# A graph network's edge sums: the first five edge tiles of every source tile moved between the scatter blocks

## The chip, the cores and the metric

The kernel runs on one core of a Trainium2 chip. The metric is the device time of one execution in microseconds: the median of three runs of the kernel before is 2264.07 us (2262.4 to 2264.69). One execution was also profiled; every row shown below is from that one. The core's engines are PE (TensorE, matrix products and transposes), DVE (VectorE), ACT (ScalarE), POOL (GpSimd) and SP (SyncE, which issues transfers here). Each engine works through its own instructions in order; a wait at the head of an engine's queue holds all that stands behind it. "PEld" in the profile is the loading of weights into TensorE.

## The reference, cut to what matters

There are N = 3125 nodes of 256 features, E = 50000 edges (src, dst), sorted by dst, and 16 features per edge. The first half is a message network, the second a graph convolution of three layers:

```python
h = relu(layernorm(x))
z = concat([h[src], h[dst], edge_attr])          # per edge
m = relu(z @ mW1 + mb1) @ mW2 + mb2              # hidden width 512
agg = segment_sum(m, src, N)                     # per source node
u = relu(concat([h, agg]) @ uW1 + ub1) @ uW2 + ub2
x = x + h + u
h = relu(layernorm(x))
# three layers: A_norm @ (h @ W_l) + b_l, gelu between them; edges and self loops
x = x + gcn(h)
```

## The kernel before

**Splitting the message.** mW1 is cut into the part for the source, the part for the destination and the part for the edge's features. The kernel makes two tables, tabA = h times the source part and tabB = h times the destination part plus mb1 (each row is kept as a rounded number and its remainder, 2 × 512 wide). A message's hidden row is relu(tabA[src] + tabB[dst] + edge part), and the sum over a source's edges is taken before mW2 is applied. 25 source tiles of 125 nodes each have 17 edge tiles of 128 places (2176 places in rows_d, each a row of 528 numbers = 2112 bytes).

**Stage one, the blocks.** In a start-up the kernel normalizes nodes (`norm`, `turn_nodes`, which also stores h to h_d), and computes for every edge its place in rows_d (lines 319 to 417: one-hots S of the source tile, counts, prefix sums, peers, place, ends). Then come 66 blocks of 768 edges, six columns of 128 edges each, in the order of dst. `window(b)` (line 526) loads 128 rows of tabB for block b, three blocks ahead; SP issues it, or ACT for every fifth block. `prepare(b)` makes the transposed features and the one-hots of the destinations (lines 540 to 555). `block(b)` makes the products p_z on PE (lines 568, 570), copies them two columns at a time into one of four buffers zt (line 573, ACT for four columns and DVE for two) and sends every column to its places with an indirect transfer from POOL (line 576, `rows_d<-zt,place`, 391 in all). These scatters are declared free of dependencies among each other (the group "rows"), since every edge has a place of its own. Between the blocks the kernel makes the remaining tables (`table`, lines 294 to 311, two chunks of 128 nodes per call), tests on the places (lines 468, 470), stores the transposed h (hT_d), and clears places that may stay empty (`fill`, line 237, two source tiles per transfer). Calls are handed out by block number: what tabB needs in blocks 0 to 17, then the tests, the tables of A and hT in blocks 18 to 61.

**Stage two, the sums** (`messages`, lines 714 to 890). For each source tile t: `load_rows` (line 728) loads its rows in five groups of three or four edge tiles, waiting for all scatters; `load_tile` loads 128 rows of tabA (apc). `one_hots` (lines 750 to 760) makes the one-hot of each edge's source (oh), its transpose (ohT) and a half-precision copy (oh_h). `edge_tile` (lines 799 to 810) picks the row of tabA with the transposed one-hot (p_x), adds the edge's row (gb, DVE), takes the relu (ACT) and the remainder (m, DVE); `sums` (line 818) adds the edge tile into p_sum with the one-hot, and at the end ACT copies p_sum to R (line 822). A list `beside` is handed out between the edge tiles: `adjacency(t - 1)`, which makes one-hots of destinations (od, line 769, DVE) and counts edges into the matrix A (p_A, line 776, and a copy to bytes, line 794), and `update(t - 1)`. The update begins with `edges_of_sources`: POOL adds the 17 one-hot tiles together (lines 832, 835, 836), and a product with a column of ones gives the number of edges of each source. `node_steps` then applies mW2, uW1, uW2. `residual` (called by `fetch`) loads x and h and has POOL add them with the bias ub2 (lines 649, 650).

**Stage three** turns the degree counts into scales and runs the three convolution layers with A (products at line 1097).

**What sets the order.** The order of instructions on each engine is the program's order as the tile framework keeps it, with the lists `of_B`, `work` and `beside` placing the side work by hand. The framework also puts in the waits: an instruction that reads what another writes waits for it, for tiles in memory off the core as well, unless the two were declared free of each other. The line that does this for the scatters, and the wait that row loads of stage two are given by hand:

```python
tc.declare_no_dep(s.ins, group="rows", reason="every edge has a place of its own")
tc.add_to_no_dep_group("rows", s.ins)
...
for s in scatters:
    tc.add_manual_dep(o.ins, s.ins.name, SYNC, reason="all rows are in place")
```

Of the kernel before, what the change touches and what calls it, by code (L numbers as in the profile page):

```python
# [54 lines left out]
EARLY, HEAD, TAIL = 24, 5 * P, 3 * P  # L56
MID = 1024
# [30 lines left out]
assert len(begun) == NG  # L88
FIRST = [v[0][1] for v in PIECES]
# [4 lines left out]
def gnn(ctx: ExitStack, tc: tile.TileContext, x, src, dst, ea, mW1, mb1, mW2, mb2, uW1, ub1, uW2,  # L94
# [11 lines left out]
            dram.tile([N - TAIL, 2 * H], F32, name="tabB1")]  # L106
    hT_d = dram.tile([P, 2, N], F32, name="hT_d")
    h_d = dram.tile([N, D], F32, name="h_d")
# [12 lines left out]
    for name, v, none in (("kr_s", src, -8000), ("kr_d", dst, 0)):  # L121
        t = l1.tile([NB, BLK], I32, name=name)
        nc.vector.memset(t[64:NB, :], none)
        nc.scalar.dma_start(t[:NB - 1, :], v[:FULL].rearrange("(b e) -> b e", e=BLK))
        nc.scalar.dma_start(
            t[NB - 1:NB, :].rearrange("b (p j) -> b p j", j=MB)[:, P - LEFT:, MB - 1:MB],
            v[FULL:].rearrange("(b p j) -> b p j", b=1, j=1))
        kr.append(t)
    xt = g1.tile([P, NR, D], F32, name="xt")
    REST = N - (NR - 1) * P  # L130
    groups = [(0, 5), (5, 13), (13, 19), (19, NR)]
    wAB = g1.tile([P, 2, 2, H], F32, name="wAB")

    def load_x(a, e):
        nc.sync.dma_start(xt[:, a:e, :], x[a * P:e * P, :].rearrange("(c p) f -> p c f", p=P))
# [7 lines left out]
    nc.sync.dma_start(bias_f, mb1.rearrange("(o f) -> o f", o=1))  # L143
# [3 lines left out]
    nc.sync.dma_start(xt[:REST, NR - 1, :], x[(NR - 1) * P:, :])  # L147
    load_w(0)
    wE4 = l1.tile([P, H], F32, name="wE4")
    for q in range(0, P, ED):  # L150
        nc.sync.dma_start(wE4[q:q + ED, :], mW1[2 * D:2 * D + ED, :])

# [60 lines left out]


    scatters = []

    with s1:
# [3 lines left out]
        def small(dtype=F32):  # L221

            turn[0] += 1
            return gps.tile([P, H], dtype, name=("tr", "bc", "p_tab")[turn[0] % 3])
# [7 lines left out]
        zero = g1.tile([P, (KT - SURE // P) * ZW], F32, name="zero")  # L232
# [3 lines left out]
        def fill(a, e, after):  # L236
            f = nc.sync.dma_start(
                rows_d[:ROWS, :].rearrange("(t s) w -> t s w", s=CAP)[a:e, SURE:, :]
                .rearrange("t (p i) w -> p t (i w)", p=P),
                zero.unsqueeze(1).to_broadcast([P, e - a, (KT - SURE // P) * ZW]))  # L240
            tc.add_manual_dep(f.ins, after.ins.name, SYNC, reason="others are wanted first")
            tc.declare_no_dep(f.ins, group="rows", reason="before its places have edges")
            tc.add_to_no_dep_group("rows", f.ins)
            fills.append(f)
# [14 lines left out]
        def norm(c0, c1):  # L259
            for c in range(c0, c1):  # L260
                n = parts(c)
                ln_stats(g1, mv[:n, c, :], xt[:n, c, :], n)
            return ln_scale(g1, mv[:, c0:c1, :], P, f"ln{c0}")

        def turn_nodes(c, e, scale, c0):

            rstd, nmr = scale
            h = g1.tile([P, 2, D], F32, name="h", bufs=3)
            p = small().rearrange("p (k a) -> p k a", k=2)
            for i in range(e - c):  # L270
                n = parts(c + i)
                nc.scalar.activation(h[:n, i, :], xt[:n, c + i, :], AF.Relu,
# [5 lines left out]
            for b, f, n in whole(c, e):  # L278
                a = (c + b) * P
                nc.sync.dma_start(  # L280
                    h_d[a:a + (f - b) * n, :].rearrange("(i p) f -> p i f", p=n), h[:n, b:f, :])
            a, b = c * P, min(e * P, N)
            nc.scalar.copy(hT[:, :, a:b], p[:, :, :b - a])


# [8 lines left out]
        def table(pool, name, s, c, e, stores, bufs=2):  # L294

            p = gps.tile([P, 2, H], F32, name="p_z", bufs=2)
            for i in range(e - c):
                n = parts(c + i)
                if s == 1:
                    nc.tensor.matmul(p[:n, i, :], ones_r[:, :n], bias, start=True, stop=False)  # L300
                for k in range(2):
                    nc.tensor.matmul(p[:n, i, :], hT[:, k, (c + i) * P:(c + i) * P + n],
                                     wAB[:, s, k, :], start=s == 0 and k == 0, stop=k == 1)
            o = pool.tile([P, 2, 2, H], F32R, name=name, bufs=bufs)
            for b, f, n in whole(c, e):
                nc.scalar.copy(o[:n, b:f, 0, :], p[:n, b:f, :])
                nc.vector.tensor_sub(o[:n, b:f, 1, :], p[:n, b:f, :], o[:n, b:f, 0, :].bitcast(F32))
                a = (c + b) * P
                for d, at in stores:
                    d = d[a - at:a - at + (f - b) * n, :].rearrange("(i p) f -> p i f", p=n)  # L310
                    nc.sync.dma_start(d, o[:n, b:f].rearrange("p i s f -> p i (s f)").bitcast(F32))
# [21 lines left out]
        nc.scalar.copy(kd, key_p[1][:, :CN])  # L333
        cs_i = l1.tile([P, CN], I32, name="cs_i")
# [5 lines left out]
        nc.vector.tensor_copy(cs, cs_i)  # L340
        S = l1.tile([P, MB, NT, NB], F16, name="S")
        for t in range(NT):
            nc.vector.tensor_scalar(S[:, :, t, :], cs_h.rearrange("p (j b) -> p j b", j=MB), float(t),
                                    None, op0=ALU.is_equal)
        own = l1.tile([P, NT * NB], F16, name="own")
# [18 lines left out]
        for t0 in range(0, NT, 2 * TG):  # L364
            p = gps.tile([P, 2, H], F32, name="p_z", bufs=2)
            for i in range(2):
                a = t0 + i * TG
                v = slice(a * NB, min(a + TG, NT) * NB)
                n = v.stop - v.start
                nc.tensor.matmul(p[:, i, :n], tri, own[:, v], start=True, stop=False)  # L370
                nc.tensor.matmul(p[:, i, :n], ones_h[:NB, :], Xv[:, v], start=False, stop=True)
                nc.vector.tensor_scalar(base[:, v], p[:, i, :n], float(-MID), None, op0=ALU.add)

        p_pos = gps.tile([P, H], F32, name="p_pos")
# [10 lines left out]
        same = l1.tile([P, CN], F16, name="same")  # L385
        for d in range(1, MB):
            n = (MB - d) * NB
            nc.vector.tensor_tensor(same[:, :n], cs_h[:, d * NB:], cs_h[:, :n], op=ALU.is_equal)
            nc.vector.tensor_add(peers[:, d * NB:], peers[:, d * NB:], same[:, :n])
        real = g1.tile([P, CN], F32, name="real")  # L390
        nc.vector.tensor_scalar(real, cs, -0.5, None, op0=ALU.is_gt)
        pos = g1.tile([P, CN], F32, name="pos")
        nc.vector.scalar_tensor_tensor(pos, real, float(MID), peers, op0=ALU.mult, op1=ALU.add)
        nc.vector.tensor_add(pos, pos, p_pos[:, :CN])

        most = l1.tile([P, MB, NB], F32, name="most")
        nc.gpsimd.memset(most, float(CAP))
        nc.gpsimd.memset(most[:, :, :FROM], float(SURE))
        okay = g1.tile([P, CN], F32, name="okay")
        nc.vector.tensor_tensor(okay, pos, most.rearrange("p j b -> p (j b)"), op=ALU.is_lt)  # L400
        nc.vector.tensor_mul(okay, okay, real)
        at = l1.tile([P, CN], F32, name="at")
        nc.vector.scalar_tensor_tensor(at, cs, float(CAP), pos, op0=ALU.mult, op1=ALU.add)
        nc.vector.tensor_mul(at, at, okay)
# [4 lines left out]
        nc.vector.scalar_tensor_tensor(spare, okay, 0.5, spare, op0=ALU.is_lt, op1=ALU.mult)  # L409
        place = g1.tile([P, MB, NB], I32, name="place")  # L410
        nc.vector.tensor_add(place.rearrange("p j b -> p (j b)"), at, spare)
        ps_f = l1.tile([P, CN], F32, name="ps_f")
        nc.vector.scalar_tensor_tensor(ps_f, cs, -float(NP), ks, op0=ALU.mult, op1=ALU.add)
        ends = g1.tile([P, MB, NB, 2], F32, name="ends")
        for i, v in enumerate((ps_f, kd)):
            nc.vector.tensor_scalar(ends[:, :, :, i], v.rearrange("p (j b) -> p j b", j=MB), 1.0, None,
                                    op0=ALU.add)


        for c, f in pairs(*groups[0]):  # L420
            turn_nodes(c, f, scales[groups[0]], 0)
        for c, f in ((0, 2), (2, 3), (3, 5)):
            table(l1, "b_sb", 1, c, f, [(tabB[0], 0)] + [(tabB[1], TAIL)] * (c >= 3))


        w0 = l1.tile([NB, 1], F32, name="w0")
        at0 = (P - LEFT) * MB + MB - 1
        nc.vector.tensor_scalar(w0, pid[:NB], float(NB - 1), krf[1][:, at0:at0 + 1], op0=ALU.is_equal,
                                op1=ALU.mult)
        nc.vector.tensor_add(w0, w0, krf[1][:, 0:1])  # L430
        w_lo = l1.tile([NB, 1], F32, name="w_lo")
        nc.vector.tensor_scalar(w_lo, pid[:NB], EARLY - 0.5, float(TAIL), op0=ALU.is_gt, op1=ALU.mult)
        w_hi = l1.tile([NB, 1], F32, name="w_hi")
        nc.vector.tensor_scalar(w_hi, w_lo, (N - HEAD) / TAIL, float(HEAD - P), op0=ALU.mult,
                                op1=ALU.add)
        nc.vector.tensor_tensor(w0, w0, w_lo, op=ALU.max)
        nc.vector.tensor_tensor(w0, w0, w_hi, op=ALU.min)
# [766 lines left out]
```

## Time and profile before

| part of the profiled execution | from, us | to, us | length, us |
|---|---|---|---|
| start-up, to the first scatter | 0 | 78.3 | 78.3 |
| blocks 0 to 25 | 79.4 | 353.6 | 274.2 |
| blocks 26 to 65 | 353.6 | 713.7 | 360.1 |
| between the last scatter and the sums | 713.7 | 738.0 | 24.3 |
| sums, 25 source tiles | 738.0 | 1660.0 | 922.0 |
| last update, degrees | 1660.0 | 1687.0 | 27.0 |
| convolution layers | 1687.0 | 2261.0 | 574.0 |
| span | | | 2261.1 |
| this execution's own time | | | 2262.93 |
| median of the runs | | | 2264.07 |

The stages were cut where a line's first or last instruction starts or ends (line 576 for the blocks, lines 750 and 822 for the sums). Over the whole span PE is busy 1910.8 us (85%), DVE 1364.2 (60%), ACT 958.7 (42%) and POOL 566.1 (25%); the shares differ much from stage to stage, so each stage is read for itself. The largest groups of instructions:

| line, engine | what | count | busy, us | mean, ns |
|---|---|---|---|---|
| L576 POOL | scatter of 128 rows | 391 | 378.4 | 968 |
| L1097 PE | convolution products | 2100 | 443.3 | 370 |
| L818 PE | sums, 512 columns | 850 | 355.9 | 458 |
| L803 PE | row of tabA, 512 columns | 850 | 337.0 | 460 |
| L808 DVE | remainder of m | 425 | 313.1 | 745 |
| L805 DVE | gb | 425 | 286.8 | 680 |
| L769 DVE | one-hots of destinations | 425 | 237.0 | 578 |
| L832 POOL | first addition of one-hot tiles | 25 | 56.8 | 2272 |

A matrix product's busy time overlaps its neighbours'; how far two are apart is read from their starts.

### The profile page before, as it was taken

The page shows a single profiled execution, that of the slowest core. Times are in us where ns is not written, and L with a number is a line of the kernel's source. Part 1 is how long each engine was busy: PE and PEld are TensorE (multiplying, and loading weights), DVE is VectorE, ACT ScalarE, POOL GpSimd, SP SyncE. Part 2 cuts the span into 40 slices and gives each one's busy share as a digit, 9 for nine tenths or more (in the row PEclk, how much of TensorE's full clock was granted, in tenths as well). Part 3 has the DMA queues.
Part 4 walks back from the last instruction along what each step waited for, and adds up shares of the span by engine and source line. Part 5 has one row for each costly group of instructions (what it writes and reads, how often), then busy time and mean ns, then how long its engine had stood idle before and what let it go on. Part 6 is the DMA issues. An engine that isn't in the chain of part 4 may idle for free. (4 is left out here: it accounts for less than half of the span.)

```text
span 2261.1 us, 27055 instructions
## 1 busy us (share of the span) xinstructions
PE 1910.8 (85%) x9215; PEld 1489.7 (66%) x9215; DVE 1364.2 (60%) x2863; ACT 958.7 (42%) x1755; POOL 566.1 (25%) x607
## 2 busy tenths in 40 slices
PE   4588767767883889999999999998978999999993
PEld 2455445544552667777777777777756998998991
DVE  8743333333431899999999999999952223223221
ACT  1333222222331555555555555555636444344430
POOL 1355466666563221221212121212100000000000
PEclk9889877789996899999999999999989999999995
DMA  3879898877996454544444444444411000000003
GB/s 127 313 283 344 289 347 305 285 245 255 340 324 221 151 166 138 166 148 153 153 153 148 163 138 165 150 154 153 143 59 50 1 1 1 1 1 1 1 4 112
DMA packets 158307, 358.91 MB, mean 159 GB/s; under 512 B 28643, under 2 KB 55685, under 8 KB 157768
## 3 DMA queue, kind: packets, MB, share of 16 engines
q1 hardware_dynamic: 111066, 235.28, 31.3%
q0 software_dynamic: 31280, 105.73, 12.3%
q10 hardware_dynamic: 15806, 16.01, 2.4%
q8 instruction: 76, 1.25, 0.2%
q14 instruction: 79, 0.65, 0.1%
HBM read 191.45 MB, written 165.44 MB: 158 GB/s over the span
## 5 line engine op out<-in xcount | busy, mean ns | idle before, releaser
L576 POOL DMA_INDIRECT rows_d<-zt,place x391 | 378.4, 968 | 269.1 <-issue 114.7
L1097 PE MATMUL p_o<-a,g 125*128 125x448 f32 x2100 | 443.3, 370 | 0.0
L1097 PEld LDWEIGHTS p_o<-a,g 125*128 125x128 f32 x2100 | 394.8, 188 | 32.5 <-ACT g L1069 0.3
L818 PE MATMUL p_sum<-m,oh 128*125 128x512 f32 x850 | 355.9, 458 | 66.0 <-DVE m L808 46.2
L807 ACT ACTIVATE m<-gb 128x512 fp32r<-128x512 f32 x425 | 265.4, 632 | 233.4 <-DVE gb L805 221.7
L803 PE MATMUL p_x<-apc,ohT 125*128 125x512 f32 x850 | 337.0, 460 | 2.3 <-DVE gb L805 1.1
L808 DVE SCALAR_TENSOR_TENSOR m<-gb,m 128x512 fp32r<-128x512 f32 x425 | 313.1, 745 | 8.2 <-ACT m L807 6.1
L805 DVE TENSOR_TENSOR gb<-z,p_x 128x512 f32<-128x512 f32 x425 | 286.8, 680 | 30.1 <-PE p_x L803 27.1
L570 PE MATMUL p_z<-bw,ohd 128*128 128x512 f32 x782 | 285.5, 449 | 0.0
L1091 DVE CAST a<-A 125x448 fp32r<-125x448 uint8 x262 | 102.9, 393 | 273.6 <-PE p_o L1097 273.5
L568 PE MATMUL p_z<-wE,payT 128*128 128x512 f32 x391 | 186.4, 477 | 76.8 <-issue 27.9
L1093 ACT CAST a<-A 125x448 fp32r<-125x448 uint8 x263 | 148.7, 566 | 240.8 <-PE p_o L1097 240.8
L776 PE MATMUL p_A<-od,oh_h 128*126 128x448 f16 (+2 forms) x1000 | 248.9, 317 | 0.0
L818 PEld LDWEIGHTS p_sum<-m,oh 128*125 128x125 f32 x850 | 154.0, 188 | 142.9 <-DVE m L808 68.3
L573 ACT COPY zt<-p_z 128x1024 f32<-128x1024 f32 x131 | 132.2, 1010 | 256.6 <-PE p_z L570 129.3
L769 DVE TENSOR_SCALAR od<-iota_h,dloc 128x896 f16<-128x896 f16 (+16 forms) x425 | 237.0, 578 | 0.3 <-PE p_A L776 0.3
L570 PEld LDWEIGHTS p_z<-bw,ohd 128*128 128x128 f32 x782 | 169.8, 218 | 76.5 <-issue 45.0
L803 PEld LDWEIGHTS p_x<-apc,ohT 125*128 125x128 f32 x850 | 153.5, 194 | 34.9 <-ACT ohT L759 9.6
L568 PEld LDWEIGHTS p_z<-wE,payT 128*128 128x128 f32 x391 | 84.8, 217 | 131.3 <-issue 56.0
L554 DVE TENSOR_SCALAR ohd<-bc,pid 128x384 fp32r<-128x384 f32 x132 | 81.0, 614 | 131.1 <-PE bc L552 61.7
L776 PEld LDWEIGHTS <-oh_h 128*126 128x126 f16 x1000 | 133.3, 136 | 37.7 <-issue 1.2
L573 DVE COPY zt<-p_z 128x1024 f32<-128x1024 f32 x65 | 79.3, 1221 | 97.3 <-remote 37.6
(225 smaller groups left out, 2263.6 us busy)
## 6 DMA issues: line engine op xcount, KB each, us to landing
z<-rows_d SPq DMA_DIRECT2D x75, 792.0 KB
z<-rows_d SPq DMA_DIRECT2D x50, 1056.0 KB
bw<-tabB SPq DMA_DIRECT2D x53, 512.0 KB
rows_d<-zero SPq DMA_DIRECT2D x12, 1584.0 KB
tabA<-t_sb SPq DMA_DIRECT2D x12, 1024.0 KB
apc<-tabA SPq DMA_DIRECT2D x24, 512.0 KB
tabB<-t_sb SPq DMA_DIRECT2D x9, 1024.0 KB
bw<-tabB ACTq DMA_DIRECT2D x13, 512.0 KB
```

The lines of the kernel that those rows point to most:

```text
L568: nc.tensor.matmul(o, pay[b][:, j // 2, :], wE[j % 2], start=True, stop=False)
L570: nc.tensor.matmul(o, one[b][:, j, :], bw[b][:, s * H:(s + 1) * H], start=False, stop=s == 1)
L573: (nc.vector.tensor_copy if j0 == 2 else nc.scalar.copy)(z[:, a:e, :H], p[:, a - j0:e - j0, :])
L576: s = nc.gpsimd.indirect_dma_start(out=rows_d, in_=z[:, j, :], in_offset=None, out_offset=bass.IndirectOffsetOnAxis(ap=place[:, j, b:b + 1 ...
L769: nc.vector.tensor_scalar(targets[k][:, :WIDTH[k]], iota_h[:, :WIDTH[k]], dloc[t][:, k:k + 1], None, op0=ALU.is_equal)
L776: nc.tensor.matmul(p_A[g][:, l - g * AW:h - g * AW], oh_h[t][:, k, :], targets[k][:, l - FIRST[k]:h - FIRST[k]], start=start, stop=stop)
L803: nc.tensor.matmul(p, ohT, apc[t][:NP, s, :], start=s == 0, stop=s == 1)
L805: nc.vector.tensor_add(gb, zr, p)
L807: nc.scalar.activation(m[:, 0, :], gb, AF.Relu)
L808: nc.vector.scalar_tensor_tensor(m[:, 1, :], gb, 0.0, m[:, 0, :].bitcast(F32), op0=ALU.max, op1=ALU.subtract)
L818: nc.tensor.matmul(p_sum[t], oh, m[:, s, :], start=k == 0 and s == 0, stop=k == KT - 1 and s == 1)
L1097: nc.tensor.matmul(po[:, f, :AW], g[:, s, q, f * P:(f + 1) * P], a, start=s == 0 and q == 0, stop=s == NT - 1 and q == 1)
```

## The change

Stage one also does the first KP = 5 of the 17 edge tiles of every source tile, in blocks FULL_AT = 26 to 65: 125 edge tiles over 40 blocks. By the kernel's own tests these five hold the edges whose destinations are small, so that blocks 0 to 25 fill them. A generator does the work, and is advanced between the blocks:

```diff
+        def rows_of(t):
+            v = g1.tile([P, XZ], F32, name="xz", bufs=2)[:, :KP * ZW]
+            v = v.rearrange("p (k w) -> p k w", w=ZW)
+            o = nc.sync.dma_start(
+                v, rows_d[t * CAP:t * CAP + KP * P, :].rearrange("(k p) w -> p k w", p=P))
+            for c in ready:
+                tc.add_manual_dep(o.ins, c.ins.name, SYNC, reason="all rows are in place")
+            a = p1.tile([P, 2, H], F32R, name="apc", bufs=2)
...
+            nc.sync.dma_start(a.rearrange("p s f -> p (s f)").bitcast(F32)[:n],
+                              tabA[t * NP:t * NP + n, :])
+            return v, a
+
+        def first_sums():
+            loaded = {0: rows_of(0)}
...
+                if k == KP - 1:
+                    r = p1.tile([NP, H], F32, name="R_part")
+                    nc.scalar.copy(r, p_s[t])
+                    nc.sync.dma_start(R_d[t * NP:(t + 1) * NP, :], r)
+            for t in range(NT):
+                if t + 1 < NT:
+                    loaded[t + 1] = rows_of(t + 1)
+                v, a = loaded.pop(t)
...
+                kept = p1.tile([P, KP, NP + 1], F16, name="oh_kept")
+                nc.scalar.copy(kept, oh.bitcast(F32))
+                nc.sync.dma_start(oh_d[t], kept.rearrange("p k n -> p (k n)"))
+                for k in range(KP):
+                    p = gps.tile([P, H], F32, name="p_x", bufs=2)
+                    new = edge_tile(p1, p, ohT[:, k, :], a, v[:, k, :H])
+                    if last is not None:
+                        add(*last)
+                    last = t, k, oh[:, k, :NP], new
+                    yield
...
+            if b == FULL_AT:
+                ready += scatters
+                sums, n_sums = first_sums(), NT * KP
             block(b)
+            for v, n in work:
+                while len(v) > max(0, n - n * (b + 1) // FULL_AT):
+                    v.pop(0)()
+            if b >= FULL_AT:
+                while n_sums > NT * KP - NT * KP * (b + 1 - FULL_AT) // (NB - FULL_AT):
+                    next(sums)
+                    n_sums -= 1
+            if 2 <= b < NT + 2:
+                fill(b - 2, begins[b])
```

So all tables, tests and hT are made by block 25, one chunk of 128 nodes per table call, and the clearing transfers go one source tile per block in blocks 2 to 26. To make room, xt becomes two halves that the rows xz take over later, zt has three buffers in place of four, p_z three single banks in place of two double ones, the features come six blocks at a time. The copies of p_z are made per column, all by ACT from block 26 on (before, DVE makes columns 2 and 3). The one-hots of these five edge tiles (half precision) go to oh_d, the partial sums to R_d, and the destinations' numbers stay on the core (d_of). The manual wait above is for the scatters of blocks before 26.

The residual x + h + ub2 is now made in `turn_nodes` by two DVE additions and stored to xs_d in place of h. In the start-up, several steps move between engines and in order: the peers' sums, `real`, `at` and `ends` go to POOL, `near` to ACT, the first tables and the windows' starts come before the one-hots S, the tests and most `norm` calls come after the first blocks.

Stage two does edge tiles 5 to 16, and has no arithmetic on POOL:

```diff
-        GROUPS = ((0, 4), (4, 8), (8, 11), (11, 14), (14, 17))
+        GROUPS = ((5, 9), (9, 13), (13, 17))
...
+                nc.sync.dma_start(oh_h[t][:, :KP, :].rearrange("p k n -> p (k n)"), oh_d[t])
...
+            def source_counts():
+                nc.tensor.matmul(p_A[g][:, AW:AW + 1], oh_h[t][:, k, :], ones_h[:, 0:1],
+                                 start=False, stop=False)
...
+            if NEW[g]:
+                nc.scalar.copy(of_src[t][:, g:g + 1], p_A[g][:NP, AW:AW + 1])
+            if g == NG - 1:
+                nc.vector.tensor_reduce(n_src[:, t:t + 1], of_src[t], axis=AX.X, op=ALU.add)
...
-                R[t] = mp.tile([NP, H], F32, name="R", bufs=2)
-                nc.scalar.copy(R[t], p_sum[t])
+                nc.vector.tensor_add(R[t], R[t], p_sum[t])
...
-            xs_t[t] = residual(mp, w, t, nc.gpsimd, 3)
+            R[t] = mp.tile([NP, H], F32, name="R", bufs=3)
+            nc.sync.dma_start(R[t], R_d[t * NP:(t + 1) * NP, :])
```

The number of edges of a source is counted on PE, with one product of a single column for each of the 17 edge tiles, into a spare column of p_A; ACT copies seven such columns out and DVE adds them. The partial sums are loaded into R, and DVE adds p_sum to them. The update of a tile comes two tiles later in place of one, and the weights of the update are loaded after the first rows.

## The prediction

> **What bounds the kernel now.** I cut the span by the order of the lines into stages and read each with the windows view (busy time and instructions of each engine, granted clock, DMA share, GB/s): blocks 0 to 25, blocks 26 to 65, the sums stage.
>
> ```profile
> 79.40:353.60 274.20, 208.54 (x739) 136.49 (x738) 108.03 (x247) 83.79 (x110) 151.81 (x157) 0.86 0.85 311
> 353.60:713.70 360.10, 271.34 (x978) 182.84 (x976) 128.75 (x235) 106.66 (x129) 225.44 (x235) 0.88 0.79 283
> 738.00:1660.00 922.00, 848.85 (x4677) 667.56 (x4676) 875.45 (x1727) 514.43 (x1034) 177.07 (x175) 0.98 0.46 149
> ```
>
> The columns are PE, PEld, DVE, ACT, POOL. In the sums stage DVE is busy 875 of 922 us: it is the bound, PE close behind. In the later blocks no engine is full; the timeline shows what paces them:
>
> ```profile
> 374.00 1.01 ACT L573 COPY zt<-p_z 128x1024 f32<-128x1024 f32 x1 [0.32 <-PE p_z L570]
> ...
> 375.21 0.96 POOL L576 DMA_INDIRECT rows_d<-zt,place  x1 [0.30 <-issue]
> ...
> 376.47 0.96 POOL L576 DMA_INDIRECT rows_d<-zt,place  x1 [0.30 <-issue]
> ...
> 377.25 0.39 PE L568 MATMUL p_z<-wE,payT 128*128 128x512 f32 x1
> ...
> 377.49 0.63 PE L570 MATMUL p_z<-bw,ohd 128*128 128x512 f32 x2
> ...
> 377.74 0.96 POOL L576 DMA_INDIRECT rows_d<-zt,place  x1 [0.30 <-issue]
> 377.95 0.40 PE L568 MATMUL p_z<-wE,payT 128*128 128x512 f32 x1
> ```
>
> Scatters start 1.27 us apart (375.21, 376.47, 377.74). 235 of them after block 25 make 298 us of the 360; 62 us are bubbles (waits for the zt copies, mostly). The PE rows give a price used below: three 512-column products from 377.25 to 377.95, 0.23 each. For blocks 0 to 25 the 156 scatters make only 198 of 274 us; with DMA at 0.85 and 311 GB/s I take transfers as their limit.
>
> How DVE loses time in the sums stage:
>
> ```profile
> 1643.17 2.20 POOL L832 TENSOR_TENSOR oh_sum<-oh_h 128x1008 f16<-128x1008 f16 x1 [31.24 <-ACT oh_h L760]
> 1643.32 2.30 DVE L769 TENSOR_SCALAR od<-iota_h,dloc 128x834 f16<-128x834 f16 x1
> ...
> 1645.45 2.65 POOL L835 TENSOR_TENSOR oh_sum<-oh_sum 128x504 f16<-128x504 f16 x3
> 1645.53 1.62 DVE L808 SCALAR_TENSOR_TENSOR m<-gb,m 128x512 fp32r<-128x512 f32 x1
> ```
>
> The 834-wide one-hot takes 2.30 us beside POOL's addition, against about 0.4 by the undisturbed form (1709 columns 0.66 us); L808 takes 1.62 against 0.68. Adding such excesses up gives 4.1 us in each source tile's 36.95 us (24 gaps between the copies of L822, 772.7 to 1659.6).
>
> **The sum, part by part**, against the profiled execution: span 2261.1 us, run 2262.93 (1.8 outside the span); the median of the runs is 2264.07, 0.05% above it.
>
> *Start-up.* The first scatter is at 78.28 now. In the new order 12 of 20 statistics of nodes and the tests stand behind it, the peers' sums go to POOL, the first table comes earlier. 12 × (0.404 + 0.163) = 6.8 us and 7 × 0.555 + 8 × 0.354 = 6.7 us leave DVE; two added additions per pair cost some 1 us back. −12; bounds −18 (more of the chain moved) and −6 (a DMA sets it).
>
> *Blocks 0 to 25.* Now they move 274 × 0.311 = 85 MB. The tables of A (12.8 MB), hT (3.2 MB) and the fills that came later (about 5.7 MB) move in: about 107 to 109 MB. At 335 GB/s (the two fullest slices of the page have 344 and 347) 325 us; at today's 311, 350; at 344, 316. +55, bounds +30 (if part of today's transfers were not the limit) and +80.
>
> *Blocks 26 to 65.* Their engines have room: 125 edge tiles over 40 blocks put PE, ACT and DVE at 7 to 10 us per block, where six scatters take 7.6 and the drains below make it 12. The price is elsewhere. Line 640 of the new kernel loads rows_d while scatters still write it. The scatters are declared free among themselves, the load is not: in the changed kernel's order of instructions each load waits on SP for the last scatter issued before it to land, and the first scatter of the following block waits on POOL for the load. The manual dependency (all scatters of blocks before 26) would ask far less. So the scatter queue is emptied 24 times (tiles 0 and 1 together). Behind the load on SP stand apc, the bw windows (three blocks ahead, so they bear it), R_d and oh_d stores; behind the held scatter stand the rest of POOL's scatters, which set the end. No wait of this kind is in the trace; its parts are. Landing: after the last scatter's issue at 713.74 the next SP transfer starts at 716.14 on its landing, and 1.2 us of this is a recorded wait: 1.4 to 3, taken 2.2. Reading: four edge tiles (512 rows × 2112 B) were issued at 800.57, and the engines worked on them to about 805.4:
>
> ```profile
> 802.00:803.00 1.00, 1.00 (x5) 0.71 (x5) 1.00 (x4) 0.00 (x0) 0.00 (x0) 1.00 0.81 165
> 803.00:804.00 1.00, 1.00 (x7) 0.83 (x7) 0.76 (x4) 0.70 (x2) 0.00 (x0) 1.00 1.04 384
> 804.00:805.00 1.00, 1.00 (x7) 0.77 (x6) 0.98 (x3) 1.00 (x3) 0.00 (x0) 1.00 1.01 367
> 805.00:806.00 1.00, 1.00 (x7) 0.73 (x6) 0.97 (x2) 0.64 (x3) 0.00 (x0) 1.00 0.42 158
> ```
>
> that is 4.8 us, and 128 rows more (0.27 MB at 370 GB/s) make 5.4. With two wakings of 0.1, less the 0.3 between scatters anyway: 7.5 a drain. 24 × 7.5 = 180, and 3.5 for the doubled first load. New: 298 + 180 + 3.5 + 12 (what I leave of the bubbles, since the drains give late copies time to arrive) = 493, so +133. The bytes allow it: 283 GB/s × 360 us = 102 MB, less the A tables, hT and fills, plus rows 33.8, apc 12.8, oh_d 4, R_d 6.4 gives about 144 MB, 430 us at 335 GB/s. Bounds: +110 (the shortest landing, no bubbles) and +170 (today's bubbles in part, landing under load).
>
> [...]
>
> *Gap before the sums* (713.7 to 738.0). The row loads stand ahead of the 2 MB of weights now; the last tile's last sums come in. −7, bounds −12 and 0.
>
> *Sums stage.* Per source tile, now 12 edge tiles. DVE: 12 × (0.60 + 0.60) = 14.4 (clean starts of gb and m), one-hots of targets 6.0, of sources 2.2, the node's 1.0, R's addition 0.6 (as gb's), counts 0.2: 24.4. The 4.1 us beside POOL are gone with POOL's work; if another cause stands behind them they stay, 28.5. PE: 48 products × 0.23 = 11.05, node steps 7.8 and transposes 1.3 (by gaps between starts), counts 6.05, 17 one-column products × 0.064 (line 351 did 25 in 1.6 us) = 1.1: 27.3. ACT about 15: it loses the R copy, gains seven small ones. So PE takes over as the bound. Today's bound, DVE, fills 95% of its stage; with that for PE 27.3 / 0.935 to 27.3 / 0.95, taken 29.2; bounds 27.5 and 31.5 (DVE bound with the stall kept, or coupling of the two). 25 × 29.2 + 32 for the first and last tile's ends = 762, against 949 (738 to 1687): −187, bounds −220 and −130. The gcn stages are untouched.
>
> Sum: −12 + 55 + 133 − 7 − 187 = −18: 2262.9 − 18 = 2245, and 2246 beside the median.
>
> **Rivals.** First, the forecast: the gain of the sums stage slightly exceeds what the blocks give back; its own range, by half the bounds of each term, 2205 to 2259. Second, on the other side: the drain costs more than I priced, at one place, the pair load 640 and the next scatter. The forecast turns at 18 / 24 = 0.75 more, 8.25 us a drain. For it: between loads 9.6 scatters, windows, apc, oh_d and R_d move 4.4 MB in some 12.2 us, 360 GB/s, above anything the page shows, so a backlog would stand before each last scatter and delay its landing; 3.5 us more each (11 us) gives 2246 + 84 = 2330, 1.5 more gives 2282. Against it: apc stands behind the row load on SP and runs while scatters have begun again. Third: PE packs better and DVE's 24.4 + 5% = 25.7 sets the tile: 25 × 3.5 = 88 less, about 2160; against it, PE's 27.3 is already made from back-to-back products. Fourth: the drains fall where the 62 us of bubbles are anyway (both come at ends of blocks), none is left and half of a drain's landing is hidden: 493 − 12 − 24 × 1.1 = 455, 2208; I count it to the forecast's sign. That one-column counts cost more than 0.064 is the small case: at 0.19 each, 2.1 us a tile, +54, on the second's side.
>
> **How the numbers follow.** Forecast 0.42, the second rival (with the last) 0.42, third and fourth together 0.16. About 0.2% (4.5 us) is what a measurement here can tell from no change; 0.06 of the forecast's share falls there. Faster 0.52, within 0.06, slower 0.42. The range leaves out the third's far end and drains above 10.5 us: 2180 to 2320.
>
> **What would show it.** In the changed profile: 24 gaps of about 7.5 us between scatters, each ended by rows loaded; scatters of the later blocks ending about 160 to 175 us later than now; no POOL arithmetic after the blocks and the 834-wide one-hot at 0.4 us; R's addition every 29 us with PE near 94%. I would be wrong on the blocks if scatters ran on through the row loads (then −180), on the sums stage if PE showed idle time behind DVE at a period above 31.5.

## The result, and the profile after

The changed kernel takes 2288.19 us (median of 5 runs, 2278.76 to 2297.84), the kernel before 2264.07 (5 runs, 2258.19 to 2266.63): 1.0105 times the time, with a 95% interval of 1.0066 to 1.0145. The change made the kernel slower by about 1% there; on another chip (e13_after below) the same two kernels are 2.9% apart. The forecast was 2246, a small gain. Of the run e7_poolcounts below, one of the four executions took 4600.51 us, about twice the other three, and is left out of its time.

The profiled execution has a span of 2296.0 us, 34.9 above the span before. The windows view, cut where stages begin and end (first scatter, first scatter of block 26, last scatter's end, first and last addition into R), tells where they come from; the columns are those of the prediction's first view:

```profile
72.07:409.36 337.29, 261.04 (x839) 155.96 (x838) 150.95 (x376) 109.66 (x203) 155.24 (x156) 0.87 0.86 317
409.36:971.80 562.44, 400.75 (x1513) 285.56 (x1512) 249.56 (x513) 267.49 (x495) 237.26 (x235) 0.82 0.71 250
971.80:1016.90 45.10, 29.65 (x145) 21.22 (x145) 29.55 (x69) 18.43 (x39) 0.02 (x1) 0.81 0.77 256
1016.90:1685.80 668.90, 663.97 (x4247) 560.79 (x4247) 593.91 (x1344) 381.01 (x865) 0.00 (x0) 0.99 0.50 158
```

The first line is blocks 0 to 25, the second blocks 26 to 65: there POOL is busy 237 of 562 us, DMA 0.71, PE 0.71, so that nothing is full. The last is the sums stage, where PE is busy 664 of 669 us. Term by term, against the prediction (the stages before are cut at the same scatters, which moves two of them by some 0.2 to 1 us against the table ahead of the prediction):

| part | before, us | after, us | difference | predicted |
|---|---|---|---|---|
| to the first scatter | 78.3 | 72.1 | -6.2 | -12 |
| blocks 0 to 25 | 274.4 | 337.3 | +62.9 | +55 |
| blocks 26 to 65 | 361.1 | 562.5 | +201.4 | +133 |
| last scatter to the convolutions | 973.3 | 750.2 | -223.1 | -194 |
| convolutions | 574 | 574 | 0 | 0 |
| sum | | | +35.0 | -18 |

One term is off by more than all others together: blocks 26 to 65. The starts of the scatters there show 24 gaps above 6 us, each between the last scatter of a block and the first of the next; together they are 253 us longer than 24 usual distances, and all other distances together only 12 us longer (before, one gap above 6 us, and 59 us in small ones). So the bubbles are what was forecast, and so is the number of drains (a drain is such a gap: the scatters' queue runs empty before the next scatter); their price is not. The waits view of the stage, for SP and POOL (total, times, longest):

```profile
SPq L640 <- DMA rows_d<-zt,place: 157.1, 20, 10.9
```

```profile
POOL rows_d L611 <- DMA xz<-rows_d: 130.8, 12, 12.2
```

SP stands at the load of rows (line 640) until scatters have landed, and POOL stands at the next scatter (line 611) until the rows are read. POOL's row has 12 of the 24 drains; the view puts the others down to another engine, as in the drain shown next, by the timelines of POOL and SP:

```profile
784.49 1.26 POOL L611 DMA_INDIRECT rows_d<-zt,place  x1 [0.30 <-ACT m L240]
794.09 1.38 POOL L611 DMA_INDIRECT rows_d<-zt,place  x1 [8.34 <-DVE m L241]
```

```profile
787.60 0.37 SPq L640 DMA_DIRECT2D xz<-rows_d  x1
791.58 0.32 SPq L646 DMA_DIRECT2D apc<-tabA  x1
```

POOL's gap is put down to DVE, whose m ended at 793.78. The semaphores in the trace tell otherwise: the one that the load issued at 787.60 raises has its last update at 793.32, and POOL's wait for it ends at 793.34. So it is in all 24 drains: POOL goes on 0.02 us after the load's last update, and the scatter starts 0.75 us later, time that goes by in the wait instructions that stand between. In windows of 1 us across it, the last two columns (DMA share, GB/s) show the transfers run dry and fill again:

```profile
786.00:787.00 1.00, 1.00 (x6) 0.81 (x5) 0.12 (x1) 1.00 (x3) 0.00 (x0) 1.00 0.67 266
787.00:788.00 1.00, 0.45 (x2) 0.01 (x1) 0.33 (x2) 1.00 (x3) 0.00 (x0) 1.00 0.02 4
788.00:789.00 1.00, 0.51 (x2) 0.46 (x3) 0.96 (x4) 0.23 (x1) 0.00 (x0) 1.00 0.44 32
789.00:790.00 1.00, 1.00 (x6) 0.78 (x6) 0.60 (x2) 0.27 (x1) 0.00 (x0) 1.00 0.75 277
790.00:791.00 1.00, 1.00 (x6) 0.82 (x5) 0.00 (x0) 0.89 (x2) 0.00 (x0) 1.00 1.02 399
```

Between 787 and 789 the 16 engines moved 36 KB. By the packets of the trace, the mean of the 23 drains after the first is: last scatter's end to its last packet 2.36 us, from there to the load's issue 0.59, issue to first packet 1.29, first to last packet 4.93, last packet to the next scatter 1.22; 10.4 in all, of which 0.3 would have passed anyway. The 1.22 are 0.45 from the last packet to the last update of the load's semaphore and the 0.77 just told. The first drain, with two loads, took 20.2, of which 9.1 are landing.

In the sums stage the one-hots of 834 columns, which took 1.28 us on average before, are back to the time of their size:

```profile
L860 DVE TENSOR_SCALAR od<-iota_h,dloc 128x1145 f16<-128x1145 f16 x23 | 11.9, 517 | 0.0
L860 DVE TENSOR_SCALAR od<-iota_h,dloc 128x834 f16<-128x834 f16 x23 | 10.0, 433 | 0.0
```

### The profile page after: what moved, and what is told of

It is laid out like the page before. It is cut to its first block, busy times and chain, and to the rows that moved or that the text cites. A ratio compares the mean times of both kernels' runs of the same rounds, so it can differ in the third digit from the quotient of the medians.

```text
span 2296.0 us, 28904 instructions
## 1 busy us (share of the span) xinstructions
PE 1943.7 (85%) x9615; PEld 1532.4 (67%) x9615; DVE 1264.2 (55%) x2886; ACT 1031.1 (45%) x2090; POOL 425.7 (19%) x450
## 3 DMA queue, kind: packets, MB, share of 16 engines
q8 instruction: 79, 1.29, 0.2%
## 5 line engine op out<-in xcount | busy, mean ns | idle before, releaser
L611 POOL DMA_INDIRECT rows_d<-zt,place x391 | 392.5, 1004 | 516.4 <-ACT zt L610 157.3
L1190 PEld LDWEIGHTS p_o<-a,g 125*128 125x128 f32 x2100 | 394.6, 188 | 32.4 <-ACT g L1162 0.2
L241 DVE SCALAR_TENSOR_TENSOR m<-gb,m 128x512 fp32r<-128x512 f32 x425 | 287.8, 686 | 47.0 <-ACT m L240 39.7
L610 ACT COPY zt<-p_z 128x512 f32<-128x512 f32 x339 | 195.6, 588 | 226.9 <-PE p_z L608 160.8
L917 PE MATMUL p_sum<-m,oh 128*125 128x512 f32 x600 | 235.0, 436 | 1.4 <-DVE R L920 0.7
L874 PE MATMUL p_A<-od,oh_h 128*126 128x448 f16 (+3 forms) x1000 | 235.2, 325 | 0.2 <-ACT of_src L905 0.2
L238 DVE TENSOR_TENSOR gb<-z,p_x 128x512 f32<-128x512 f32 x300 | 202.0, 681 | 31.0 <-PE p_x L236 28.7
L236 PEld LDWEIGHTS p_x<-apc,ohT 125*128 125x128 f32 x850 | 164.0, 207 | 29.9 <-DVE gb L238 8.9
L659 PE MATMUL p_sum<-m,oh 128*125 128x512 f32 x250 | 106.2, 471 | 51.3 <-DVE m L241 27.8
L860 DVE TENSOR_SCALAR od<-iota_h,dloc 128x447 f16<-128x447 f16 (+11 forms) x300 | 138.5, 486 | 0.0
L917 PEld LDWEIGHTS p_sum<-m,oh 128*125 128x125 f32 x600 | 112.4, 189 | 38.4 <-ACT m L240 15.5
L238 DVE TENSOR_TENSOR gb<-xz,p_x 128x512 f32<-128x512 f32 x125 | 83.5, 684 | 78.0 <-PE p_x L236 51.7
```

Of the source, the lines that this page charges most:

```text
L236: nc.tensor.matmul(p, ohT, apc[:NP, s, :], start=s == 0, stop=s == 1)
L238: nc.vector.tensor_add(gb, zr, p)
L241: nc.vector.scalar_tensor_tensor(m[:, 1, :], gb, 0.0, m[:, 0, :].bitcast(F32), op0=ALU.max, op1=ALU.subtract)
L610: (nc.vector.tensor_copy if b < FULL_AT and j in (2, 3) else nc.scalar.copy)(z[:, j, :H], p)
L611: s = nc.gpsimd.indirect_dma_start(out=rows_d, in_=z[:, j, :], in_offset=None, out_offset=bass.IndirectOffsetOnAxis(ap=place[:, j, b:b + 1 ...
L874: nc.tensor.matmul(p_A[g][:, l - g * AW:h - g * AW], oh_h[t][:, k, :], targets[k][:, l - FIRST[k]:h - FIRST[k]], start=start, stop=stop)
```

## The experiments

The runs were made on several chips, each beside the kernel before on the same chip. That kernel took 2264 to 2273 us on some and 2226 to 2229 on one (the runs e10 to e16), while the changed kernel took 2288 and, on that one, 2289. So ratios to the kernel before are compared within a chip, and stages from the traces. The numbers in brackets are 95% intervals of the ratio.

**e1_free: the row loads freed from the scatters of later blocks.** The load joins the group of the scatters; what it must wait for (all scatters of blocks 0 to 25) is given once, by way of a tiny DVE instruction outside the group.

```diff
+            if t == 0:
+                g_ = p1.tile([1, 1], F32, name="gate")
+                x_ = nc.vector.memset(g_, 0.0)
+                for c in ready:
+                    tc.add_manual_dep(x_.ins, c.ins.name, SYNC, reason="all rows are in place")
+                gate0.append(x_)
+            tc.add_manual_dep(o.ins, gate0[0].ins.name, SYNC, reason="all rows are in place")
+            tc.declare_no_dep(o.ins, group="rows", reason="later blocks write other rows")
+            tc.add_to_no_dep_group("rows", o.ins)
```

> The changed kernel, its row loads freed from the scatters of later blocks (they still wait for all scatters of blocks 0 to 25, once). Theory, the emptied queue: the 24 gaps (10.4 us each from the last scatter's end to the next scatter, 253 us above the usual distance in all) vanish, no load follows a landing any more; blocks 26 to 65 fall from 561 us to 430-450, where 144 MB at 335 GB/s become the limit, and the run from 2288 to about 2160 (2140-2190). Rival, transfers: the gaps only show that the transfers are full; the scatters wait elsewhere, blocks 26 to 65 stay above 520 us and the run above 2245.

Measured: 2179.14 us, 0.9583 [0.9548, 0.9618] of the kernel before. The stages of its trace:

```profile
70.40:409.00 338.60, 262.53 (x839) 155.15 (x838) 150.41 (x376) 109.89 (x203) 154.54 (x156) 0.86 0.87 316
409.00:851.50 442.50, 357.41 (x1501) 263.59 (x1501) 244.35 (x508) 262.03 (x493) 232.93 (x235) 0.93 0.89 317
```

Blocks 26 to 65 fall from 562 to 442.5 us, with DMA up from 0.71 to 0.89; blocks 0 to 25 are as they were. The theory's numbers hold. The drains cost 120 us of this stage (109 of the run, on two chips), not the 253 of their gaps. With them gone, other waits come to light: the distances between scatters are now 146 us above the usual, where the changed kernel has 12 beside its drains. POOL's longest wait there is for ACT's copies:

```profile
POOL rows_d L611 <- ACT zt L610: 153.8, 62, 17.9
```

What holds ACT's copies back in turn, transfers (0.89) or PE (0.81 busy), is not shown.

**e2_extra: 15 more drains.** In each later block without a row load, SP reads 64 bytes of rows_d.

```diff
+                if len(calls) == had and b < NB - 1:
+                    one_row = p1.tile([1, 16], F32, name="one_row")
+                    nc.sync.dma_start(one_row, rows_d[0:1, :16])
```

> The changed kernel with 15 more drains: in each later block without a row load, SP reads 64 bytes of rows_d, which waits for the scatters and holds the next ones. Theory: a drain has a fixed price, landing 2.4 + waking SP 0.6 + issue and start 1.3 + waking POOL 1.2 = 5.5 us, whatever is read; 15 of them add 80 us (70-100), run about 2370. Rival, transfers: the scatters make up for it while the row loads move, less than 30 us are added.

Measured: 2363.95 us, 1.0415 [1.0389, 1.0441]. Blocks 26 to 65 take 631.7 us from first to last scatter, 70.6 more than in the changed kernel: 4.7 us for a drain in which hardly anything is read (from the end of one scatter to the start of the next, the 15 take 4.65 us on average). That is the theory, a little below its 5.5. So roughly half of a drain's 10.4 us is there before any rows are counted.

**e3_counts17: the kernel before, with only the counts changed.** The one-column products and their copies are those of the change; POOL's additions are gone, the residual is added by DVE.

```diff
-            xs_t[t] = residual(mp, w, t, nc.gpsimd, 3)
+            xs_t[t] = residual(mp, w, t, nc.vector, 3)
...
+            if k in NEW[g] and not start:
+                source_counts()
...
-                node = update(t - 1)
+                node = update(t - 2) if t > 1 else []
```

> The kernel before with only the counts changed: one-column products on PE, the residual's two additions on DVE, no POOL arithmetic in the sums, all 17 edge tiles there. Theory, that DVE loses 4.1 us a tile beside POOL's additions: a tile falls from 36.95 to 33.5-34.5 us, where PE (31.3 + 1.1 by starts, at 95%) sets it, the run to 2175-2205. Rival, that the long DVE instructions have another cause: a tile stays at 36.5-38 us and the run at 2255-2290.

Measured: 2228.57 us, 0.9819 [0.9795, 0.9844]; a source tile takes 35.36 us in place of 36.95. The mechanism is the expected one: the 834-wide one-hot falls from 1282 to 435 ns,

```profile
L769 DVE TENSOR_SCALAR od<-iota_h,dloc 128x834 f16<-128x834 f16 x24 | 30.8, 1282 | 0.0
```

```profile
L770 DVE TENSOR_SCALAR od<-iota_h,dloc 128x834 f16<-128x834 f16 x24 | 10.4, 435 | 0.0
```

(the first from the kernel before, the second from this run). DVE is busy 32.4 us a tile in place of 35.2, though it has two additions of the residual more (0.84 us), so some 3.7 of the 4.1 us are found. The time won is between the two expectations, about half of the theory's, because PE needs more than the 32.4 us worked out: it is busy 826 of 848.5 us at 35.36 a tile. What DVE's added residual costs beside that is not tested.

**e7_poolcounts: e1_free with POOL's additions back, no one-column products.**

> e1_free with the number of edges of a source added up on POOL again (as in the kernel before), no one-column products; the residual stays where it is. Theory, DVE loses time beside POOL: its 24.7 us a tile grow by 3.5 to 28.2 and by the waits that follow, a tile takes 29-30.5 in place of 27.9, run 2205-2245. Rival, with 12 edge tiles DVE has the room: PE loses 17 products, 1.1 us a tile, run about 2155-2175.

Measured: 2229.82 us, 0.9839 [0.98, 0.9878]; 30.43 us a tile in place of 27.90. The 1145-wide one-hot is at 1528 ns again (517 without POOL), DVE at 667 of 730 us. Theory held: the counts on PE are worth 2.5 us a tile, some 60 us, in e1_free.

The run also tells which one-hots are slowed: those that run beside an addition. POOL's additions fall elsewhere in a tile than in the kernel before, and now it is the 1433-wide one-hot that they meet (23 of 25, and none before). The first line is from the kernel before, the second from this run:

```profile
L769 DVE TENSOR_SCALAR od<-iota_h,dloc 128x1433 f16<-128x1433 f16 x24 | 14.2, 594 | 0.0
```

```profile
L868 DVE TENSOR_SCALAR od<-iota_h,dloc 128x1433 f16<-128x1433 f16 x23 | 36.0, 1567 | 0.0
```

**e4_fills2: 20 MB more in blocks 2 to 26.** Every clearing transfer is made a second time, into memory of its own.

```diff
+            nc.sync.dma_start(
+                waste[t * (CAP - SURE):(t + 1) * (CAP - SURE), :].rearrange("(i p) w -> p i w", p=P),
+                zero.unsqueeze(1).to_broadcast([P, KT - SURE // P, ZW]))
```

> The changed kernel, with every clearing transfer of blocks 2 to 26 made a second time into a memory of its own (25 x 811 KB = 20 MB more, no work for any engine but SP's issue). Theory, that blocks 0 to 25 are limited by bytes at some 317 GB/s: they grow from 337 to about 400 us (390-410), the run from 2288 to about 2350. Rival, that the smaller tables and the order of SP's queue cost the 63 us: there is room for transfers, the blocks grow by less than 25 us.

Measured: 2316.06 us, 1.0224 [1.018, 1.0267]. Blocks 0 to 25 take 342.6 us, 5 more than without, at 333 GB/s; the first drain behind them 35.5 in place of 21.2 between its scatters. The theory's number fell; the rival's held (less than 25 us), its reason in part: there was room for a third of the bytes in these blocks (114 MB moved, 107 without), and what went past them made the first rows late.

**e8_before_zt3: the kernel before with three buffers zt.** (`zt[b % 3]`, three tiles made.)

> The kernel before with three buffers zt in place of four, nothing else. In the changed kernel DVE waits 76 us of blocks 0 to 25 at line 603 for scatters to land before it may write into a buffer again (45 in the kernel before, line 560). Theory, that the lost fourth buffer is a good part of the 63 us: blocks 0 to 25 grow from 274 us by 20-45, blocks 26 to 65 by some 10-30, run 2295-2335. Rival, that the tables' work makes the 63 us: the blocks change by less than 10 us, run 2255-2275.

Measured: 2270.23 us, 1.0023 [1.0006, 1.0041]; blocks 0 to 25 in 275.8 us. The lost buffer costs next to nothing in the kernel before; that theory fell.

**e5_jit: the table of the sources made tile by tile in the later blocks** (e1_free otherwise).

```diff
-            a = p1.tile([P, 2, H], F32R, name="apc", bufs=2)
...
+            for k in range(2):
+                nc.tensor.matmul(p[:NP, :], hT[:, k, t * NP:(t + 1) * NP], wAB[:, 0, k, :],
+                                 start=k == 0, stop=k == 1)
+            a = g1.tile([P, 2, H], F32R, name="t_sb", bufs=2)
```

> e1_free, with the table of the sources made tile by tile in the later blocks, right where the sums need it, kept on the core and stored for the sums stage; it isn't loaded back there (12.8 MB less in all), and no such table is made in blocks 0 to 25. Theory, bytes: stage one loses 12.8 MB / 318 GB/s = 40 us, blocks 0 to 25 falling from 339 to about 300; run from 2179 to about 2140 (2130-2155). Rival, the engines' order: the products and copies of the table now stand in the chain of the later blocks (1.8 us of PE, 0.6 of ACT, 0.7 of DVE per source tile), what the early blocks gain is lost there; run above 2165.

Measured: 2184.83 us, 0.9644 [0.9605, 0.9682], no gain over e1_free. Blocks 0 to 25 fall to 280 us, blocks 26 to 65 grow to 502:

```profile
67.40:347.50 280.10, 210.26 (x748) 135.07 (x746) 134.25 (x352) 96.59 (x180) 152.68 (x156) 0.86 0.92 332
347.50:849.80 502.30, 409.27 (x1591) 287.85 (x1591) 258.18 (x531) 275.93 (x515) 233.20 (x235) 0.91 0.80 280
```

12.8 MB fewer to move, and nothing won: 25 tables cost some 60 us wherever they are made. That is the rival's outcome, and the reason to look at PE. e6_jit6 moves six edge tiles from block 31 on (KP = 6, FULL_AT = 31):

> e5_jit with six edge tiles of every source tile moved, from block 31 on. By e3_counts17 and the changed kernel an edge tile costs the sums stage (35.36 - 27.87) / 5 = 1.5 us, 37 us over 25 source tiles; in stage one its rows are 6.8 MB, 21 us at 318 GB/s. Theory, bytes against PE: 16 us better than e5_jit (5-25). Rival: 150 edge tiles in 35 blocks make engines the limit there, equal to e5_jit or slower.

Measured: 2201.89 us, 0.9714 [0.9671, 0.9757]: a source tile of the sums takes 26.86 us in place of 27.96, but the scatters end 51 us later. That is the rival's outcome. And e9_jit_zt4 gives e5_jit a fourth buffer:

> e5_jit with four buffers zt again (room comes from the table that isn't loaded back, and from single buffers for oh and ohT of the moved tiles). Theory of e8: DVE no longer stands at line 603 before the sums' work and the copies behind it; the 14 gaps of some 10 us in the later blocks of e5_jit go, stage one falls from 782 us to 700-740, run from 2185 to 2105-2145. Rival, that bytes or the single buffers hold it: run above 2165.

Measured: 2193.69 us, 0.9693 [0.9661, 0.9724]; blocks 26 to 65 at 505 us, and DVE still waits 93 us there at line 603 for scatters to land (79 in e5_jit). The fourth buffer, paid for with single buffers for oh and ohT, wins nothing; whether the single buffers hide a gain is not separated.

**e10_half and e11_twice, e14_half and e15_twice: the tables' products halved and enlarged.** Half leaves out features 128 to 255 of every table, twice adds features 0 to 127 once more; the tables and the outputs are not the reference's then.

```diff
-            for k in range(2):
+            for k in range(1):
                 nc.tensor.matmul(p[:n, :], hT[:, k, c * P:c * P + n], wAB[:, s, k, :],
-                                 start=k == 0, stop=s == 0 and k == 1)
+                                 start=k == 0, stop=s == 0)
```

> The changed kernel, whose tables are made from the first 128 of the 256 features alone (half of the product is left out): 42 us less of PE in blocks 0 to 25, everything else the same, bytes, copies, SP's order. Theory, that PE paces blocks 0 to 25 (busy 0.77 of them, 0.76 in the kernel before, 0.75 in e5_jit): they fall from 337 us by 42/0.77 = 55 to 275-300, run 2288 to 2230-2250. Rival, that the table's chain of copies and SP's queue paces them: less than 15 us.

> The changed kernel, with the first half of every table's product added twice (the tables are then not the reference's): 42 us more of PE in blocks 0 to 25, all else the same. Theory, PE: blocks 0 to 25 grow from 337 us by 40-60, run 2330-2350. Rival: less than 15 us.

Measured: 2255.57 us, 1.0131 [1.011, 1.0151], and 2302.78 us, 1.0323 [1.0294, 1.0353]; blocks 0 to 25 in 287.0 and 349.5 us. On this chip the kernel before took 2228.58, so a control was needed, and all three ran again beside each other:

> The changed kernel itself, as the control for the three beside it on one chip: blocks 0 to 25 in 325-340 us, run 1.0066 to 1.0145 times the kernel before.

> e10_half beside the control: the tables from the first 128 features alone, 42 us less of PE in blocks 0 to 25, nothing else. Theory, PE paces these blocks: 35-60 us less than the control there, and as much in the run. Rival, the chain of copies and SP's queue: less than 15 us. Third, transfers: less than 15 us as well, with the DMA share up to 0.94.

> e11_twice beside the control: 42 us more of PE in blocks 0 to 25. Theory, PE: 35-60 us more than the control there and in the run. Rival: less than 15 us.

Measured: 2289.32 us, 1.0286 [1.0255, 1.0317] for the changed kernel; 2248.49, 1.0113 [1.0073, 1.0152] with half; 2297.95, 1.0313 [1.0283, 1.0343] with twice. Blocks 0 to 25 of the three (the changed kernel, half, twice):

```profile
68.30:399.90 331.60, 256.08 (x838) 153.99 (x837) 150.41 (x376) 109.84 (x203) 153.91 (x157) 0.88 0.88 322
```

```profile
67.30:358.10 290.80, 223.45 (x747) 136.47 (x746) 147.78 (x372) 109.18 (x203) 155.28 (x156) 0.86 0.95 346
```

```profile
71.60:422.00 350.40, 290.38 (x926) 173.15 (x925) 147.77 (x369) 109.95 (x204) 154.37 (x157) 0.89 0.84 305
```

The control's blocks are as expected, its ratio to the kernel before is not, since that kernel is faster on this chip. Half the products: 41 us less there and 41 less in the run, as PE's theory has it, with PE busy 33 us less; and DMA goes to 0.95 and 346 GB/s. More products: 19 us more, between the theories, and 9 in the run. So the products of the tables are a large part of what these blocks grew by, but PE alone is not the limit. That PE (0.77) and DMA (0.88) share it is read from these shares and not tested further.

**e12_kp4: e1_free with four edge tiles moved, from block 21 on** (KP = 4, FULL_AT = 21).

> e1_free with four edge tiles of every source tile moved, from block 21 on. The sums stage grows by 25 x 1.5 = 37 us. Theory, PE paces both stages: stage one loses 25 edge tiles at some 1.3-1.5 us of PE and its waits, 33-40 us; the run stays within 15 us of e1_free (2179). Rival, that the moved tiles find free time in stage one: the run is 25 us or more above e1_free.

Measured: 2192.62 us, 0.9848 [0.9829, 0.9867] of the kernel before on the faster chip. The sums take 29.58 us a tile, and the scatters end at 823 us in place of 852. e16_lead, beside a kernel before of nearly the same time (2226.44), is 20 us faster, of which some 7 are its own gain over e1_free; so four tiles are by this estimate some 13 us slower than five, on the theory's side of the line, across two groups of runs.

**e16_lead: e1_free with its first rows asked for two blocks ahead of the first sums.**

```diff
-            loaded = {0: rows_of(0)}
+            loaded = {0: rows_of(0), 1: rows_of(1)}
             p_s, last = {}, None
+            yield
...
+            if b == FULL_AT:
+                next(sums)
-            if b >= FULL_AT:
+            if b >= FULL_AT + 2:
```

> e1_free, whose first two row loads are issued after block 26 while the first sums start only after block 28. Theory: the gap of 18.8 us at the first sums is the way of the first rows (DVE waits 17.3 us for them); it goes, run 10-18 us below e1_free's 0.958 of the kernel before (0.951 to 0.955). Rival: the 125 tiles in 38 blocks in place of 40 give it back: 0.956 to 0.960.

Measured: 2172.59 us, 0.9765 [0.9735, 0.9795] of the kernel before on its chip, where the changed kernel takes 2289.32: 0.949 of the changed kernel (e1_free: 2179.14 / 2288.19 = 0.952, on two chips). The gap of 18.8 us is gone (the longest is now 10.0), blocks 26 to 65 take 435.7 us. The expected ratios were for a chip with the slower time before; against the changed kernel some 7 us are won, as blocks 26 to 65 show too (442.5 in e1_free), where 10 to 18 were expected. It is the fastest version here, below both kernels in the runs beside it.

## Why the prediction was wrong

**The step that failed** is the price of a drain, in the term of blocks 26 to 65: "With two wakings of 0.1, less the 0.3 between scatters anyway: 7.5 a drain." The runs show 10.1. Landing was priced at 2.2 and took 2.36; waking SP at 0.1 and took 0.59; the load at 5.4 from issue to last packet and took 6.2; waking POOL at 0.1 and took 1.22. The two wakings alone make 1.6 of the 2.6 us missing. No row of the profile before shows the 0.1. The price had no row for the time between the last packet of a transfer and the instruction that waits for it, and I put in a small number where a bound from both sides was due. The waking itself is short, 0.02 us on POOL; what was left out is the 0.45 from the last packet to the last update of the semaphore, on both sides, and the 0.75 of POOL's further wait instructions. The rows themselves moved at 274 GB/s, where the price had 370 for its last part. 24 × 2.6 = 62, and with the first drain 70: the whole error of the term, and enough to turn the sign (the point of turning was given as 8.25).

The Trainium skill, "DMA: Bandwidth & Descriptors", section "Anatomy of one DMA — SWDGE (gpsimd) path", gives a transfer issued by GpSimd a fixed cost of about 2.0 us beside its bytes, most of it after the data, until the write is confirmed. A scatter is such a transfer; the row load, issued by SP, is not. An estimate by the page's fit, used for both, is 2.6 us for a scatter (0.27 MB) and 5.1 us for a row load (1.35 MB), 7.7 us one after the other; these runs show 10.4, and the measurement decides. That most of the fixed cost stands behind the data is not seen in the row loads here: 1.29 us pass from the issue to the first packet, 0.45 from the last packet to the last update of the semaphore.

**The rival on the other side** had the right place and the wrong reason: it expected a backlog of bytes before each last scatter. Landing took 1.4 to 4.2 us, 2.36 on average, and only at the first drain 9.1; the price came from what stands around the packets and from the load's way.

**That the scatters would be held at all**, 24 times, by waits that the framework puts in beside the ones given by hand, was right, and e1_free shows it: with those waits gone, 120 us of the stage are. That only 12 us of bubbles would be left beside the drains, since late copies get time to arrive, has its reason confirmed there (146 us without the drains); that the number came out to the microsecond is luck.

**Blocks 0 to 25**: +55 forecast, +63 measured, right in size and not in its reason. "Transfers as their limit" fails: the stage ran at 317 GB/s, not 335, and 346 was to be had (e14_half). PE's part, the tables' products, wasn't in the sum at all; halving them gave back 41 us, and without the 25 tables of A (e5_jit) the stage takes 280 us, close to the 274 before. The sum had a slip as well: 107 to 109 MB at 335 GB/s make 319 to 325 us, a growth of 45 to 51 and not 55. (So has the check on bytes in the later blocks: its parts make 137 MB, not 144; 140 were moved.)

**Sums stage**: -194 forecast with the gap before it, -223 measured. PE took over as forecast, at 27.87 us a tile, not 29.2. PE's sum of 27.3 was near; the 94 to 95% by which I divided it was not, since PE is busy 99% here. In e3_counts17 the same sum was 3 us short, so its closeness is partly luck. The stall beside POOL was read rightly (e3_counts17, e7_poolcounts).

**The scatters themselves** kept their time beside DVE's added work: a scatter's median is 960 ns after as it was 961 before, though its mean rose from 968 to 1004.

**Start-up**: -12 forecast, -6 measured, at the bound given.

What stays open: why the kernel before is 1.6 to 2.1% faster on one of the chips, while the changed one is not; and what besides PE and transfers holds blocks 0 to 25.

## What to carry to other kernels

Here each load that read where another queue still wrote emptied that queue, though the two never touched the same rows: look in the order of the built program for what each transfer really waits for, not at the waits written by hand. Price such a handover with what stands around the data, the landing, the way to the issue, the issue and the way back to the waiting engine (here 5.5 of 10.4 us), and count how often it happens. And when work is moved into "free" time, price every engine there, not only the one that looked full.

## What the runs showed of the hardware

From the last packet of a row load to the start of the scatter that waited for it 1.22 us pass: 0.45 to the last update of the load's semaphore, 0.02 to the end of POOL's wait, and 0.75, the same in all 24 drains, in POOL's further wait instructions. From the last packet of a scatter to the load's issue 0.59 us pass. A drain in which 64 bytes are read costs 4.7 us.

POOL's additions in half precision slow DVE's one-hots that run beside them. In the kernel before, the 1145-wide one takes 2252 ns on average in the 16 source tiles where it overlaps an addition and 519 in the other 9; the 834-wide one takes 1282 with and 435 without (e3_counts17); the 1433-wide one takes 594 where it meets none and 1567 in e7_poolcounts, where it meets them. The kernel before ran 1.6 to 2.1% faster on one chip than on the others, while the changed kernel did not (2288 and 2289 us).
